# Re-ordering the first two rows of a three-stage macaron block: turned-tile copies as a step of their own, stores on ScalarE, three chunks kept on chip

## The chip, the core and the metric

The kernel runs on one core of a Trainium2 chip. The metric is device time in microseconds (us) of one execution, taken as the median of several runs. The engines have the profile's names: PE is TensorE, DVE is VectorE, ACT is ScalarE, POOL is GpSimd, SP is the sync engine, which in this kernel only issues transfers. Each engine works through its own queue in order.

## The reference

Eight rows (batch entries) of 512 tokens by 512 features go through feed-forward, attention, feed-forward, each with a layer norm before it and a residual around it. The change touches the first feed-forward. Cut to that:

```python
def ternary_quant(w, g=64):                      # per group of 64, in bf16
    scale = clip(mean(abs(w_g)), 1e-8)
    return clip(round(w_g / scale), -1, 1) * scale
def ffn(x, w_gate_up, w_proj):                   # hidden width 2048
    gate, up = split(x @ ternary_quant(w_gate_up).T, 2)
    h = silu(gate) * up
    h = h * rsqrt(mean(h * h) + eps)             # rms norm over the hidden width
    return h @ ternary_quant(w_proj).T
x = x + 0.5 * ffn(layernorm(x), w_gate_up, w_proj)
x = x + sliding_window_attention(layernorm(x))   # 32 heads, window 128
x = x + 0.5 * ffn(layernorm(x), w_gate_up, w_proj)
```

## The kernel before

Three stages follow one another: feed-forward "a", attention "b", feed-forward "c". Tiles with `_a` and `_c` in their names belong to the two feed-forwards. In a feed-forward the hidden width is cut into 16 chunks of 128 (`FC` = 16). For one row and chunk, `gate_or_up` (L283) makes gate and up with eight matmuls of 128x512 each (the normalised row is held as two terms, a rounded high one and the low rest). `silu` (L296) runs on ScalarE, `product` (L301) multiplies on VectorE into `h`. `high_term` (L306, ScalarE) and `low_term` (L311, VectorE) split `h` into `hs`, and `project` (L319) adds the chunk to the four output tiles with eight matmuls. The rms norm is a factor per token, so it is applied at the end, in `finish` (L335), from sums of the squares of `h`. All of the first stage's matmuls of the second and later rows find the quantised weights on chip.

The first two rows are different: `first_rows` (L362) quantises the weights while it computes rows 0 and 1. A class `Quantised` (L114) holds the steps for one weight tile. There are 16 gate/up tiles (`g[c]`, one a chunk) and 8 projection tiles (`pr[u]`, one for two chunks), each 128 partitions by 1024. The steps are `load` (DMA issued by SP), `magnitude` and `sign` (ScalarE), `scales` (VectorE, group means), `spread` (ScalarE, means copied to the groups' width, written to `step`), `first_half` and `second_half` (VectorE, five operations, giving `wt`), and `turned`: eight transposes on TensorE into a PSUM tile, its copy to the weight tile by ScalarE, and a store of that tile to DRAM for stage "c", issued by SP.

In `first_rows` the order on PE, DVE and ACT is the order of the program text (`manual_schedule`, L370); SP and POOL are ordered by the planner. The main loop (L422) runs over `c`. Pass `c` computes chunk `c` of row 0 and chunk `d = c - BEHIND` of row 1, with `BEHIND` = 5; it quantises tile `g[c + 1]` to its end and begins `g[c + 2]`, and works on one projection tile for each two passes. Row 0's sums of squares are made by four small matmuls a pass into the PSUM tile `ms_first` (L474). Row 0's projection runs `LAG` = 2 passes behind. Row 1's own layer norm is spread over the first passes (`norms[1]`: statistics, scaling, and the transposes with their copies). Row 1's `h` goes to DRAM (`h_kept`, L464), because the projection of row 1 can start only when row 0's outputs have left their four PSUM banks. After the loop a second loop (L494) reads those 16 chunks back, splits them and projects them, while row 2's layer norm is made beside it.

PSUM is full: four banks of outputs, two of gate and up, and two of a pool `ps_tr` for everything turned. `ms_first` holds one of these two for the whole of the loop. `work_tile` (L293) gives five 128x512 buffers for silu, `h`, squares and read-back chunks; `hs` has three.

The middle of pass `c` reads, in the order in which the engines get it:

```python
if not odd and 0 < u <= FC // 2:
    pr[u - 1].turned()
if d >= 0:
    up1 = gate_or_up(1, d, 1)
if c < FC:
    if c + 1 < FC:
        g[c + 1].turned()
    low_term(h0, hs[c])
    sq0 = work_tile("sq", 0, c)
    nc.scalar.activation(sq0, h0, AF.Square)
```

Of the kernel before, what the change touches and what calls it, by code (L numbers as in the profile page):

```python
# [24 lines left out]
def macaron_block(  # L25
# [88 lines left out]
    class Quantised:  # L114
# [59 lines left out]
        def turned(self):  # L174
            pt = self.ps_tr.tile(
                [P, len(self.blocks), P], BF16, tag="tr", name=f"ptq_{self.name}"
            )
            for n, (i, k) in enumerate(self.blocks):
                nc.tensor.transpose(pt[:, n, :], self.wt[:, i, k * P : (k + 1) * P], ident16)
            nc.scalar.copy(self.dst, pt)  # L180
            nc.sync.dma_start(self.kept, self.dst.bitcast(F32))

    def quantise_gate_up(stage, ps_tr, wgu, c):
        src = w_gate_up.rearrange("(i c p) d -> c p i d", i=2, p=P)[c]
# [62 lines left out]
    def ffn_stage(kind, source, target, first):  # L247
# [68 lines left out]
                ps_acc.tile([P, D], F32, tag="acc", name=f"o_{kind}{b}_{t}") for t in range(TB)  # L316
            ]

        def project(ops, e, hs):  # L319
            for t in range(TB):  # L320
                for part in range(2):
                    nc.tensor.matmul(  # L322
                        ops[t], hs[:, part, t * P : (t + 1) * P], wp[e // 2][:, e % 2, :],
                        start=(e == 0 and part == 0), stop=(e == FC - 1 and part == 1),
                    )

        def sums_of(b, sumsq):
# [4 lines left out]
                )  # L332
            return ms

        def finish(b, ops, ms):  # L335

            xt = xts[b]
            var = small.tile([P, TB], F32, tag="var", name=f"var_{kind}{b}")
            nc.vector.tensor_scalar(var, ms, 1.0 / FF, RMS_EPS, ALU.mult, ALU.add)
            rms = small.tile([P, TB], F32, tag="rstd", name=f"rms_{kind}{b}")  # L340
            inv_sqrt(rms, var)
            half = small.tile([P, TB], F32, tag="half", name=f"half_{kind}{b}")
            nc.vector.tensor_scalar(half, rms, 0.5, None, ALU.mult)
# [18 lines left out]
        def first_rows():  # L362


            BEHIND = TB + 1
            own = ExitStack()
            ms = ps_tr.tile([P, TB], F32, tag="tr", name="ms_first")
            stage = own.enter_context(tc.tile_pool(name="stage", bufs=1))
            engines = {
                mybir.EngineType.PE, mybir.EngineType.DVE, mybir.EngineType.Activation,  # L370
            }
            own.enter_context(tc.manual_schedule(engines=engines))
            g = [quantise_gate_up(stage, ps_tr, wgu, c) for c in range(FC)]
# [17 lines left out]
            def normed(b, t):  # L391

                if t < TB:
                    norms[b][1](t)
                if t >= 1:
                    norms[b][2](t - 1)

            row_loaded(0)
            waiting.pop(0).load()
            waiting.pop(0).load()  # L400
            row_loaded(1)
            for t in range(TB):
                norms[0][0](t)
            begun(g[0])
            g[0].scales()
            g[0].spread()
            for t in range(TB + 1):
                normed(0, t)
                if t == 1:
                    begun(g[1])  # L410
                if t == 2:
                    g[0].first_half()
            g[0].second_half()
            g[0].turned()
            g[1].scales()
            g[1].spread()
            begun(pr[0])

            ops = outputs(0)
            sumsq = work.tile([P, T], F32, tag="ss", name="ss_second", bufs=1)  # L420
            hs, square = {}, None
            for c in range(FC + BEHIND):  # L422
                u, odd, d = c // 2, c % 2 == 1, c - BEHIND
                if c < FC:
                    gate0 = gate_or_up(0, c, 0)
                    up0 = gate_or_up(0, c, 1)
                    if c + 2 < FC:
                        g[c + 2].magnitude()
                    sg0 = silu(0, c, gate0)
                    if c + 2 < FC:  # L430
                        signed(g[c + 2])
                    if c + 1 < FC:
                        g[c + 1].first_half()
                        g[c + 1].second_half()
                    h0 = product(0, c, up0, sg0)
                    hs[c] = high_term(0, c, h0)
                    if odd:
                        pr[u].first_half()
                    else:
                        pr[u].scales()  # L440
                if d >= 0:
                    gate1 = gate_or_up(1, d, 0)
                if not odd and 0 < u <= FC // 2:
                    pr[u - 1].turned()
                if d >= 0:
                    up1 = gate_or_up(1, d, 1)
                if c < FC:
                    if c + 1 < FC:
                        g[c + 1].turned()
                    low_term(h0, hs[c])  # L450
                    sq0 = work_tile("sq", 0, c)
                    nc.scalar.activation(sq0, h0, AF.Square)
                    if c + 2 < FC:
                        g[c + 2].scales()
                if d >= 0:
                    sg1 = silu(1, d, gate1)
                if c < FC:
                    if not odd:
                        pr[u].spread()
                    if c + 2 < FC:  # L460
                        g[c + 2].spread()
                if d >= 0:
                    h1 = product(1, d, up1, sg1)
                    nc.sync.dma_start(h_kept[d], h1)  # L464

                    square = sumsq if d == 0 else work_tile("sq", 1, d)
                    nc.scalar.activation(square, h1, AF.Square)
                if c < FC:
                    if odd:
                        pr[u].second_half()  # L470
                        if u + 1 < FC // 2:
                            begun(pr[u + 1])
                    for t in range(TB):
                        nc.tensor.matmul(  # L474
                            ms[:, t : t + 1], sq0[:, t * P : (t + 1) * P], ones,
                            start=(c == 0 and t == 0), stop=(c == FC - 1 and t == TB - 1),
                        )
# [10 lines left out]
                if d >= 1:  # L488
                    nc.vector.tensor_tensor(sumsq, sumsq, square, ALU.add)


            ops = outputs(1)
            kept, terms = {}, {}
            for e in range(-4, FC):  # L494
                if e + 4 < FC:
                    kept[e + 4] = work_tile("back", 1, e + 4)
                    nc.sync.dma_start(kept[e + 4], h_kept[e + 4])
                if 0 <= e + 2 < FC:
                    terms[e + 2] = high_term(1, e + 2, kept[e + 2])
                    low_term(kept.pop(e + 2), terms[e + 2])  # L500
                if e >= 0:
                    project(ops, e, terms.pop(e))
                if e == 1:
                    stored(0)
                    ms = sums_of(1, sumsq)
                spread_norm(2, e, 2)
            finish(1, ops, ms)
            own.close()

        def row(b):  # L510
# [3 lines left out]
            for c in range(FC + LAG):  # L514
# [20 lines left out]
            finish(b, ops, sums_of(b, sumsq))  # L535
            stored(b)

        if first:
# [340 lines left out]
```

## Time and profile before

| | us |
|---|---|
| median of 3 runs (2542.94 to 2548.51) | 2548.26 |
| the profiled execution | 2547.95 |
| its span, first to last instruction | 2546.1 |
| busy in the span: PE, DVE, ACT, POOL | 2440.0, 1324.2, 983.5, 909.2 |
| gate and up matmuls of stage "a" (2048) | 493.7 |
| projection matmuls of stage "a" (1024) | 269.4 |
| weight tile store, issue to landing, median | 2.6 |
| `h_kept` store and `back` load, issue to landing, median | 2.0, 3.4 |

A row of the profile names the engine, the source line, the operation and `out<-in`; "idle before" is the time in which that engine did nothing ahead of the row, followed by what ended it. Matmuls overlap, so busy time divided by count is the cost of one (493.7 / 2048 = 0.241 us), while the mean duration that the page lists is longer. The granted clock is the share of full speed that TensorE was given. DMA share is the mean busy share of the core's 16 DMA engines. `ptq` are turned weight tiles, `ptn` turned tiles of the layer norm, `wgu` and `wp` the weight tiles, `o` outputs.

### The profile page before, as it was taken

Reading aid. Unit: us, or ns where it says so; the run is one execution under the profiler, and the core shown is the slowest. Engines: PE = TensorE matmul, PEld = TensorE weight load, DVE = VectorE, ACT = ScalarE, POOL = GpSimd, SP = SyncE. Lnnn points to the kernel's source line nnn. Section 1 sums busy time; section 2 is a strip of 40 time slices with the busy share of each in tenths; the row PEclk is TensorE's granted clock in tenths of the full one; section 3 lists DMA queues with packets and bytes.
Section 4 is the critical chain, followed back from the end, with each engine's and each line's share of the span. In section 5 each row is a group of like instructions: output and inputs, shape, how many; then the busy total and the mean of one; then the engine's idle time right before and its main releaser. Section 6 shows DMA issues by size and latency. Waiting matters only on the chain.

```text
span 2546.1 us, 40511 instructions
## 1 busy us (share of the span) xinstructions
PE 2440.0 (96%) x16184; PEld 1788.0 (70%) x16184; DVE 1324.2 (52%) x3803; ACT 983.5 (39%) x1476; POOL 909.2 (36%) x778
## 2 busy tenths in 40 slices
PE   4889999999999999999999999998899999999998
PEld 3677788888888555555555555555688888888887
DVE  6665544434443466666666666665334444443442
ACT  5564322222222155555555555555222222222221
POOL 0000154444445233333333333333245445444444
PEclk9889999999999999999999999999899999999999
DMA  4332400000011100010110000022400000000000
GB/s 149 108 136 87 144 6 34 33 1 34 34 50 66 50 2 22 22 35 19 38 35 22 18 22 18 22 91 73 145 1 34 34 22 13 34 33 1 34 17 17
DMA packets 43564, 111.65 MB, mean 44 GB/s; under 512 B 3440, under 2 KB 7536, under 8 KB 40304
## 3 DMA queue, kind: packets, MB, share of 16 engines
q1 hardware_dynamic: 33392, 83.90, 9.2%
q10 hardware_dynamic: 9984, 25.17, 3.0%
q8 instruction: 127, 2.08, 0.4%
q14 instruction: 61, 0.50, 0.1%
HBM read 67.11 MB, written 41.94 MB: 43 GB/s over the span
## 4 chain that ended last, share of the span: by engine, by line
PE 92%; DVE 3%; ACT 2%; DMA 1%; issue 1%; POOL 0%; SPq 0%; POOLq 0%; DVEq 0%; ACTq 0%
PE gu_c L287 18%; PE gu_a L287 18%; PE o_a L322 10%; PE o_c L322 9%; PE sm L665 5%; PE sp L697 5%; PE wk L611 5%; PE av L733 4%; PE wq L611 4%; PE wo L611 4%; PE wv L611 4%; PE abT L751 1%; PE neg L683 1%; PE ptn_a L232 1%; PE ptn_b L232 1%
## 5 line engine op out<-in xcount | busy, mean ns | idle before, releaser
L287 PE MATMUL gu_a<-xs_a,wgu_a 128*128 128x512 f32 x2048 | 493.7, 395 | 1.8 <-ACT wgu_a L180 1.1
L287 PE MATMUL gu_c<-xs_c,wgu_c 128*128 128x512 f32 x2048 | 490.9, 393 | 0.7 <-ACT xs_c L235 0.7
L717 POOL TENSOR_SCALAR_AFFINE_SELECT pT<-pT 128x1024 f32<-128x1024 f32 x224 | 241.7, 1099 | 594.6 <-ACT pT L712 594.6
L287 PEld LDWEIGHTS gu_a<-xs_a,wgu_a 128*128 128x128 f32 x2048 | 387.7, 191 | 83.4 <-ACT wgu_a L180 1.4
L287 PEld LDWEIGHTS gu_c<-xs_c,wgu_c 128*128 128x128 f32 x2048 | 383.6, 189 | 79.8 <-ACT xs_c L235 0.9
L674 DVE CUSTOM_DVE_ANT_0 seen<-sm,window 128x256 f32<-128x256 f32 (+1 forms) x1024 | 331.6, 387 | 144.7 <-PE sm L665 143.1
L322 PE MATMUL o_a<-wp_a,hs_a 128*128 128x512 f32 x1024 | 269.4, 410 | 4.7 <-ACT hs_a L308 4.7
L322 PE MATMUL o_c<-wp_c,hs_c 128*128 128x512 f32 x1024 | 251.5, 389 | 0.0
L531 POOL TENSOR_TENSOR sq_c<-h_c 128x512 f32<-128x512 f32 x120 | 124.9, 1041 | 316.0 <-DVE h_c L303 302.5
L322 PEld LDWEIGHTS o_a<-wp_a,hs_a 128*128 128x128 f32 x1024 | 201.6, 199 | 47.9 <-ACT hs_a L308 5.2
L303 DVE TENSOR_TENSOR h_c<-gu_c,sg_c 128x512 f32<-128x512 f32 x128 | 88.2, 689 | 281.3 <-PE gu_c L287 280.1
L710 ACT ACTIVATE pT<-sp 128x512 f32<-128x512 f32 (+1 forms) x384 | 181.1, 547 | 129.5 <-PE sp L697 129.5
L303 DVE TENSOR_TENSOR h_a<-gu_a,sg_a 128x512 f32<-128x512 f32 x128 | 88.3, 690 | 262.6 <-PE gu_a L287 236.4
L712 ACT ACTIVATE pT<-pT 128x2048 f32<-128x2048 f32 (+1 forms) x128 | 217.3, 1698 | 7.9 <-DVE pT L706 3.9
L322 PEld LDWEIGHTS o_c<-wp_c,hs_c 128*128 128x128 f32 x1024 | 192.2, 188 | 39.9
L532 POOL TENSOR_TENSOR ss_c<-ss_c,sq_c 128x512 f32<-128x512 f32 x120 | 192.1, 1601 | 8.9
L298 ACT ACTIVATE sg_c<-gu_c 128x512 f32<-128x512 f32 x128 | 76.5, 598 | 264.8 <-PE gu_c L287 249.4
L308 ACT CAST hs_c<-h_c 128x512 fp32r<-128x512 f32 x128 | 79.5, 621 | 250.1 <-DVE h_c L303 250.1
L531 POOL TENSOR_TENSOR sq_a<-h_a 128x512 f32<-128x512 f32 x90 | 94.1, 1045 | 228.9 <-DVE h_a L303 219.9
L298 ACT ACTIVATE sg_a<-gu_a 128x512 f32<-128x512 f32 x128 | 76.4, 597 | 237.5 <-PE gu_a L287 228.7
L312 DVE TENSOR_TENSOR hs_c<-h_c,hs_c 128x512 fp32r<-128x512 f32 x128 | 124.0, 969 | 83.1 <-ACT hs_c L308 83.1
L308 ACT CAST hs_a<-h_a 128x512 fp32r<-128x512 f32 x112 | 69.5, 621 | 210.9 <-DVE h_a L303 210.9
(136 smaller groups left out, 3110.5 us busy)
## 6 DMA issues: line engine op xcount, KB each, us to landing
wf_gu<-w_gate_up_dram SPq DMA_DIRECT2D x16, 512.0 KB, 3.6
wgu_kept<-wgu_a SPq DMA_DIRECT2D x16, 512.0 KB, 2.6
rows_a<-x_a ACTq DMA_DIRECT2D x8, 1024.0 KB, 4.0
x_b<-rows_a SPq DMA_DIRECT2D x8, 1024.0 KB, 5.0
xr<-rows_a ACTq DMA_DIRECT2D x32, 256.0 KB, 3.1
rows_b<-xr SPq DMA_DIRECT2D x32, 256.0 KB, 2.4
x_c<-rows_b SPq DMA_DIRECT2D x8, 1024.0 KB, 4.8
wgu_c<-wgu_kept SPq DMA_DIRECT2D x16, 512.0 KB, 6.4
```

What stands on the lines that cost most here:

```text
L287: nc.tensor.matmul(ps, wgu[c][:, i * DC + k, :], xss[b][:, part, k, :], start=(k == 0 and part == 0), stop=(k == DC - 1 and part == 1),)
L298: nc.scalar.activation(sg, gate, AF.Silu)
L303: nc.vector.tensor_tensor(h, up, sg, ALU.mult)
L308: nc.scalar.copy(hs[:, 0, :], h)
L322: nc.tensor.matmul(ops[t], hs[:, part, t * P : (t + 1) * P], wp[e // 2][:, e % 2, :], start=(e == 0 and part == 0), stop=(e == FC - 1 and ...
L531: nc.gpsimd.tensor_tensor(sq, h, h, ALU.mult)
L532: nc.gpsimd.tensor_tensor(sumsq, sumsq, sq, ALU.add)
L611: nc.tensor.matmul(ps, lhs, rhs, start=(n == 0), stop=(n == len(pairs) - 1))
L674: nc.vector.tensor_tensor_reduce(out=seen[:, : n * P], in0=tiles[g][:, h, : n * P], in1=window[:, (2 - n) * P :], scale=-1.0, scalar=3.4e3 ...
L710: nc.scalar.activation(under, tiles[g][:, :, : n * P], AF.Relu, scale=-1.0)
L712: nc.scalar.activation(seen, seen, AF.Exp, scale=-1.0)
L717: nc.gpsimd.affine_select(out=half, in_=half, compare_op=ALU.is_ge, fill=0.0, base=0, pattern=[[0, 2 * NG], [sign, P]], channel_multiplier ...
```

## The change

`turned` keeps only the transposes. A new step `copied` does the copy, and the store is issued by ScalarE:

```diff
             for n, (i, k) in enumerate(self.blocks):
                 nc.tensor.transpose(pt[:, n, :], self.wt[:, i, k * P : (k + 1) * P], ident16)
-            nc.scalar.copy(self.dst, pt)
-            nc.sync.dma_start(self.kept, self.dst.bitcast(F32))
+            self.pt = pt
+
+        def copied(self):
+            nc.scalar.copy(self.dst, self.pt)
+            nc.scalar.dma_start(self.kept, self.dst.bitcast(F32))
```

The first weight tile is loaded ahead of x, its quantising comes ahead of the row's normalising, and `ms_first` is taken only after that:

```diff
-            BEHIND = TB + 1
+            BEHIND = TB + 2
-            ms = ps_tr.tile([P, TB], F32, tag="tr", name="ms_first")
...
+            waiting.pop(0).load()
             row_loaded(0)
             waiting.pop(0).load()
-            waiting.pop(0).load()
+            begun(g[0])
             row_loaded(1)
+            g[0].scales()
+            g[0].spread()
+            begun(g[1])
+            begun(pr[0])
             for t in range(TB):
                 norms[0][0](t)
-            begun(g[0])
-            g[0].scales()
-            g[0].spread()
-            for t in range(TB + 1):
-                normed(0, t)
-                if t == 1:
-                    begun(g[1])
-                if t == 2:
-                    g[0].first_half()
+            g[0].first_half()
             g[0].second_half()
             g[0].turned()
-            g[1].scales()
+            g[0].copied()
+            for t in range(TB + 1):
+                if t < TB:
+                    norms[0][1](t)
+                if t == TB:
+                    g[1].scales()
+                if t > 0:
+                    norms[0][2](t - 1)
             g[1].spread()
-            begun(pr[0])
+            ms = ps_tr.tile([P, TB], F32, tag="tr", name="ms_first")
```

In the main loop the square and the low term of row 0 move up, and the copies move down, behind the spreads (`KEPT` is 3). Row 1's transposes come one pass after their scaling. The running sum of row 1's squares (`squares_added`) is added in the pass after:

```diff
                     hs[c] = high_term(0, c, h0)
+                    sq0 = work_tile("sq", 0, c)
+                    nc.scalar.activation(sq0, h0, AF.Square)
                     if odd:
                         pr[u].first_half()
                     else:
                         pr[u].scales()
+                    low_term(h0, hs[c])
+                squares_added()
+                if 0 <= c - 2 < TB:
+                    norms[1][2](c - 2)
                 if d >= 0:
                     gate1 = gate_or_up(1, d, 0)
                 if not odd and 0 < u <= FC // 2:
                     pr[u - 1].turned()
                 if d >= 0:
                     up1 = gate_or_up(1, d, 1)
-                if c < FC:
-                    if c + 1 < FC:
-                        g[c + 1].turned()
-                    low_term(h0, hs[c])
-                    sq0 = work_tile("sq", 0, c)
-                    nc.scalar.activation(sq0, h0, AF.Square)
-                    if c + 2 < FC:
-                        g[c + 2].scales()
+                if c + 1 < FC:
+                    g[c + 1].turned()
                 if d >= 0:
                     sg1 = silu(1, d, gate1)
+                if not odd and 0 < u <= FC // 2:
+                    pr[u - 1].copied()
                 if c < FC:
                     if not odd:
                         pr[u].spread()
                     if c + 2 < FC:
+                        g[c + 2].scales()
                         g[c + 2].spread()
                 if d >= 0:
                     h1 = product(1, d, up1, sg1)
-                    nc.sync.dma_start(h_kept[d], h1)
+                if c + 1 < FC:
+                    g[c + 1].copied()
...
+                    if d >= FC - KEPT:
+                        terms[d] = high_term(1, d, h1)
+                        low_term(h1, terms[d])
+                    else:
+                        nc.scalar.dma_start(h_kept[d], h1)
...
-                if 1 <= c <= TB:
+                if 0 <= c - 1 < TB:
                     norms[1][1](c - 1)
-                    norms[1][2](c - 1)
...
                 if c == FC + LAG:
-                    finish(0, ops, ms)
+                    factor = rms(0, ms)
+                if c == FC + LAG + 1:
+                    finish(0, ops, factor)
```

`rms` is the first half of the old `finish`, the factor per token. After the loop row 1 is projected in another order: first the three chunks whose terms stayed on chip, then the 13 from DRAM, three loads ahead. The sums of row 1 and its factor come in steps 3 and 4 of that loop, where both stood before at step 1 and at the end:

```diff
-            for e in range(-4, FC):
-                if e + 4 < FC:
-                    kept[e + 4] = work_tile("back", 1, e + 4)
-                    nc.sync.dma_start(kept[e + 4], h_kept[e + 4])
...
+            order = [*range(FC - KEPT, FC), *range(FC - KEPT)]
+            for n in range(KEPT):
+                kept[n] = work_tile("back", 1, n)
+                nc.sync.dma_start(kept[n], h_kept[n])
+            for n, e in enumerate(order):
+                if n >= 1 and n + 2 < FC:
+                    ahead = order[n + 2]
+                    terms[ahead] = high_term(1, ahead, kept[ahead])
+                    low_term(kept.pop(ahead), terms[ahead])
...
+                project(ops, e, terms.pop(e), order[0], order[-1])
```

`project` takes the first and last chunk of that order, for the start and stop of the accumulation.

More of the change, by code (lines that the diff above doesn't have):

```diff
@@ L317, in outputs, with project @@
             ]
-        def project(ops, e, hs):
+        def project(ops, e, hs, begin=0, end=FC - 1):
             for t in range(TB):
@@ L323, in project @@
                         ops[t], hs[:, part, t * P : (t + 1) * P], wp[e // 2][:, e % 2, :],
-                        start=(e == 0 and part == 0), stop=(e == FC - 1 and part == 1),
+                        start=(e == begin and part == 0), stop=(e == end and part == 1),
                     )
@@ L333, in sums_of, with rms, finish @@
             return ms
-        def finish(b, ops, ms):
-            xt = xts[b]
+        def rms(b, ms):
             var = small.tile([P, TB], F32, tag="var", name=f"var_{kind}{b}")
             nc.vector.tensor_scalar(var, ms, 1.0 / FF, RMS_EPS, ALU.mult, ALU.add)
-            rms = small.tile([P, TB], F32, tag="rstd", name=f"rms_{kind}{b}")
-            inv_sqrt(rms, var)
+            factor = small.tile([P, TB], F32, tag="rstd", name=f"rms_{kind}{b}")
+            inv_sqrt(factor, var)
+            return factor
+        def finish(b, ops, factor):
+            xt = xts[b]
             half = small.tile([P, TB], F32, tag="half", name=f"half_{kind}{b}")
-            nc.vector.tensor_scalar(half, rms, 0.5, None, ALU.mult)
+            nc.vector.tensor_scalar(half, factor, 0.5, None, ALU.mult)
             for t in range(TB):
@@ L389, in signed, with squares_added @@
                     waiting.pop(0).load()
[L391 to L396, printed above, removed]
+            waiting.pop(0).load()
             row_loaded(0)
             waiting.pop(0).load()
-            waiting.pop(0).load()
+            begun(g[0])
             row_loaded(1)
+            g[0].scales()
+            g[0].spread()
+            begun(g[1])
+            begun(pr[0])
             for t in range(TB):
                 norms[0][0](t)
-            begun(g[0])
-            g[0].scales()
-            g[0].spread()
-            for t in range(TB + 1):
-                normed(0, t)
-                if t == 1:
-                    begun(g[1])
-                if t == 2:
-                    g[0].first_half()
+            g[0].first_half()
             g[0].second_half()
             g[0].turned()
-            g[1].scales()
+            g[0].copied()
[6 more added lines that the diff above has]
+                    norms[0][2](t - 1)
             g[1].spread()
-            begun(pr[0])
+            ms = ps_tr.tile([P, TB], F32, tag="tr", name="ms_first")
             ops = outputs(0)
             sumsq = work.tile([P, T], F32, tag="ss", name="ss_second", bufs=1)
-            hs, square = {}, None
+            hs, kept, terms, squares = {}, {}, {}, []
+            def squares_added():
+                if squares:
+                    nc.vector.tensor_tensor(sumsq, sumsq, squares.pop(), ALU.add)
+            KEPT = 3
             for c in range(FC + BEHIND):
@@ L463, in first_rows @@
                     h1 = product(1, d, up1, sg1)
-                    nc.sync.dma_start(h_kept[d], h1)
-                    square = sumsq if d == 0 else work_tile("sq", 1, d)
-                    nc.scalar.activation(square, h1, AF.Square)
+                if c + 1 < FC:
+                    g[c + 1].copied()
+                if d >= 0:
+                    if d == 0:
+                        nc.scalar.activation(sumsq, h1, AF.Square)
+                    else:
+                        squares.append(work_tile("sq", 1, d))
+                        nc.scalar.activation(squares[0], h1, AF.Square)
+                    if d >= FC - KEPT:
+                        terms[d] = high_term(1, d, h1)
+                        low_term(h1, terms[d])
+                    else:
+                        nc.scalar.dma_start(h_kept[d], h1)
                 if c < FC:
@@ L486, in first_rows @@
                 if c == FC + LAG:
-                    finish(0, ops, ms)
-                if d >= 1:
-                    nc.vector.tensor_tensor(sumsq, sumsq, square, ALU.add)
+                    factor = rms(0, ms)
+                if c == FC + LAG + 1:
+                    finish(0, ops, factor)
+            squares_added()
             ops = outputs(1)
-            kept, terms = {}, {}
-            for e in range(-4, FC):
-                if e + 4 < FC:
-                    kept[e + 4] = work_tile("back", 1, e + 4)
-                    nc.sync.dma_start(kept[e + 4], h_kept[e + 4])
[L498 to L503, printed above, removed]
+            order = [*range(FC - KEPT, FC), *range(FC - KEPT)]
[7 more added lines that the diff above has]
+                    low_term(kept.pop(ahead), terms[ahead])
+                    if ahead + KEPT < FC - KEPT:
+                        kept[ahead + KEPT] = work_tile("back", 1, ahead + KEPT)
+                        nc.sync.dma_start(kept[ahead + KEPT], h_kept[ahead + KEPT])
+                project(ops, e, terms.pop(e), order[0], order[-1])
+                if n == 1:
                     stored(0)
+                if n == 3:
                     ms = sums_of(1, sumsq)
-                spread_norm(2, e, 2)
-            finish(1, ops, ms)
+                if n == 4:
+                    factor = rms(1, ms)
+                spread_norm(2, n, 2)
+            finish(1, ops, factor)
             own.close()
@@ L534, in row @@
                     project(ops, c - LAG, hs.pop(c - LAG))
-            finish(b, ops, sums_of(b, sumsq))
+            finish(b, ops, rms(b, sums_of(b, sumsq)))
             stored(b)
```

## The prediction

> **What bounds the kernel now.** I read the page's rows by slice first: TensorE is at 9 tenths in nearly all of the 40 slices, and the weak ones are at the start. So I cut the span where the first two rows end: the matmuls of row 2 begin at 306.77 us on the chain of waits. A table by stretch (columns: length, busy of TensorE, weight load, VectorE, ScalarE, GpSimd with instruction counts, granted clock, DMA share, GB/s):
>
> ```profile
> 25.80:109.40 83.60, 60.35 (x273) 49.20 (x274) 58.92 (x98) 50.58 (x63) 2.89 (x4) 0.80 0.32 117
> 109.40:244.60 135.20, 120.52 (x594) 97.32 (x593) 86.59 (x134) 76.22 (x101) 0.00 (x0) 0.91 0.32 117
> 244.60:306.80 62.20, 56.73 (x258) 45.88 (x257) 29.04 (x52) 19.04 (x31) 2.88 (x3) 0.97 0.40 131
> ...
> 306.80:2546.00 2239.20, 2197.20 (x15040) 1591.82 (x15039) 1135.20 (x3486) 827.87 (x1270) 900.70 (x762) 0.99 0.10 33
> ```
>
> After 306.8 TensorE is busy 98% at a clock of 0.99, and the change touches none of it: I carry those 2239 us over. Everything is decided before. There TensorE idles 83.60 - 60.35 = 23.3, 135.20 - 120.52 = 14.7 and 62.20 - 56.73 = 5.5 us, and part of its busy time runs at a low clock.
>
> The timeline of one loop pass (start, length, what; in brackets the idle time before it and what ended it):
>
> ```profile
> 129.58 0.62 PE L179 MATMUL ptq_gu<-ident,q_wt_gu 128*128 128x128 bf16 x8
> ...
> 130.24 1.01 ACT L180 CAST wgu_a<-ptq_gu 128x1024 fp32r<-128x1024 bf16 x1 [2.56 <-PE ptq_gu L179]
> ...
> 131.15 0.63 ACT L452 ACTIVATE sq_a<-h_a 128x512 f32<-128x512 f32 x1
> ...
> 131.83 1.05 PE L474 MATMUL ms_first<-ones,sq_a 128*128 128x1 f32 x8 [1.63 <-ACT sq_a L452]
> ...
> 132.75 3.59 PE L322 MATMUL o_a<-wp_a,hs_a 128*128 128x512 f32 x8
> ```
>
> The turned weight tile is copied, only then is row 0's product squared, and TensorE stands 1.63 us because its next instruction sums those squares. ScalarE had idled 2.56 us before the copy: the square waited for its place in the queue, not for data. Then eight projection matmuls take 3.59 us, against 1.96 in undisturbed passes. The clock says why (busy of TensorE, clock):
>
> ```profile
> 130.00:132.00 2.00, 0.37 (x6) 1.00 0.00 0
> 132.00:134.00 2.00, 2.00 (x11) 0.74 0.72 291
> 134.00:136.00 2.00, 2.00 (x6) 0.50 0.27 102
> ```
>
> In the passes ahead of row 1 (c = 0 to 4) the gaps are larger:
>
> ```profile
> 56.12 0.61 PE L179 MATMUL ptq_gu<-ident,q_wt_gu 128*128 128x128 bf16 x8 [1.95 <-ACT wp_a L180]
> ...
> 71.31 1.71 PE L474 MATMUL ms_first<-ones,sq_a 128*128 128x1 f32 x8 [2.48 <-ACT sq_a L452]
> ...
> 75.95 1.09 PE L232 MATMUL ptn_a<-ident,xn_a 128*128 128x128 f32 x4 [2.94 <-DVE xn_a L224]
> ...
> 272.85 5.68 PE L322 MATMUL o_a<-wp_a,hs_a 128*128 128x512 f32 x16 [4.75 <-ACT hs_a L308]
> ```
>
> The third is row 1's transpose, queued on TensorE in the pass in which VectorE only just makes its input. The fourth is the end of the loop: row 1's first chunk is fetched from DRAM behind the last store.
>
> **The passes c = 6 to 15, both rows running.** At full clock a pass costs what the chain shows for one without a gap: 32 gate and up matmuls 7.26, sums 0.79, projection 1.97 = 10.02; plus 0.48 where a gate/up tile is turned (not in c = 15), plus 0.46 for a projection tile in even passes. Ten passes: 100.2 + 9 x 0.48 + 5 x 0.46 = 106.8 us. They took 135.2: 14.7 idle and about 13.7 of low clock and handing over.
>
> The square now follows the high term directly, ahead of the sums by row 1's up matmuls (1.9 us): this gap goes. What is late next is the tile copy, now behind the spreads and followed by the next pass's gate matmuls. Even pass, 0 = gate start, with the spacing of back-to-back rows: up ends at 3.65; VectorE's product, behind 3.4 us of quantising, ends at 4.6; high term 5.2, square 5.7, row 1's silu 6.2, projection copy 7.2, its store's issue 7.6, two spreads 9.6 (the second needs VectorE's scales, about 8.6), copy 10.6. TensorE gets there at 10.96: 0.3 us of cover. Turning both weight tiles shares one free buffer, since the sums hold the other; the projection copy ends at 7.2, and the second turn is due at 7.7. Loads of two passes: TensorE 21.5; VectorE (2 x 3.4 quantising, 2 x 1.4 scales, 8 x 0.65 for products, low terms and sums, 4.7 for the projection tile) 19.5; ScalarE 16.4 plus issues. TensorE stays the bound; I allow 0.4 us a pass for handing over: 111 us, **24 less**.
>
> Here a rule speaks against. The Trainium skill, "TensorE: Matmul & The Clock Gate", section "Why this matters for your kernels", wants no TensorE gap above about 3 us; by it a gap of 1.63 costs no clock, and the passes would fall only by their 14.7 us idle, to 120.5. The row shows the clock at 0.50 right after 1.63 us of idle and 1.05 us of matmuls one column wide. I take the row.
>
> **Stores on ScalarE.** 24 weight stores and 13 of row 1 leave SP's queue; 3 stores and 3 loads vanish. The issue is 0.32 to 0.34 us on SP and 0.33 for ScalarE's own row store. 37 x 0.33 = 12 us go to an engine 56% busy in the loop. Behind a store on ScalarE stand the spread or the next magnitude; the spread's readers are next pass's quantising and, after it, the copy. A weight store also waits for its own copy; I charge about 0.5 us each, inside the sum above. Whether a store also waits for an older transfer no ScalarE row here shows: from nothing to a full landing of 2.6 us (the weight store's median). I take nothing, since the built order asks only for transfers some passes old. SP gains: loads no longer stand behind a store waiting for ScalarE, but outside the start no magnitude waited for its weights, so 0. The skill ("DMA: Bandwidth & Descriptors", "Issuing engines are not separate DMA queues") would charge only issue time on whichever sequencer; the sum would then be 0 with ScalarE under its limit.
>
> **The start.** The first weights landed at 8.9, behind x; loaded first, with the 3.6 us of such a load, at about 4.5. Then VectorE is the line: scales to 6.9, statistics and the constants to 11.2, quantising 14.6, then four normalise, copy and low-term steps in turn with TensorE and ScalarE, and the second tile's scales (1.4) ahead of the last low term: 23.7 against 25.77, **2 less**. If ScalarE, which now takes the third tile's magnitude and sign before the first copy, must wait for that load (it cannot land much before 10.8), this gain halves.
>
> **The passes c = 0 to 5.** Row 1 starts a pass later, so six passes instead of five run without it, with nothing to cover the new order. c = 0: up ends 6.15 after the gate start (cold clock, as now); product 0.7; projection scales 1.35; low term 0.65; scales 1.35; spread 1.0; copy 1.0: the next gate starts 12.3 after, where it took 10.0. **That pass loses 2.3.** The later ones gain, because the transpose's input is a pass old. c = 3: 12.0 for up end + product 0.7, first half 1.35, two low terms 1.3, turn 0.6, what is left of the scales beside it 0.8, spread and copy 2.0 = 6.8, plus some 5 us for gate and up partly at half clock; it took 15.9. In even passes transposed tile, projection tile and gate/up tile go through the one buffer in turn, about 14. Gate starts:
>
> | pass | 0 | 1 | 2 | 3 | 4 | 5 | 6 |
> |---|---|---|---|---|---|---|---|
> | now | 25.8 | 35.8 | 48.8 | 64.4 | 80.3 | 95.4 | 109.4 |
> | estimate | 23.7 | 36.0 | 47.5 | 62.5 | 74.5 | 88.5 | 100.5 |
>
> Gaps of 3 us remain here, so I leave the clock at half for part of each. Bounds on this stretch: no gain at all (9 worse), or warm clock (5 better).
>
> **The end.** c = 16 to 21: six passes of row 1 at 3.63, two projections 1.97 each, one turn 0.46: 26.2. Row 0's finish (half and four VectorE steps, 2.9) now also has a low term before it, and the next product waits: 1.5 on TensorE, where 0.72 shows now. Then 16 projections at 1.84, sums 0.8 and four transposes at 0.44: 32.0. Sum 59.7 against 62.2 now. The 4.75 us go (three chunks are on chip, 3 x 1.84 = 5.5 us cover the 2.8 us fetch), but one more pass stands there. **2.5 less.**
>
> **Sum.** 100.5 + 111 + 59.7 = 271.2 against 306.8: 35.6 less. The profiled execution took 2547.95 (span 2546.1); the median of the runs is 2548.26, the same for this purpose. 2548 - 36 = **2512**; its own range 2502 to 2526.
>
> **Rivals.**
> - *Late copies* (18%): the 0.3 us cover is too thin, each pass stands some 1.6 us for its weight tile. Ten times 1.6 is 16: 2528. For it: the copy is last in a ScalarE chain of eight steps; against: ScalarE has 5 us in two passes free.
> - *All gaps go* (13%): the early passes also stay warm and the handing over costs nothing: 5 + 4 + 1.5 less, some 2501. Against: VectorE's chain is unavoidable in c = 0 to 5.
> - *Stores hold ScalarE* (5%), the slower side. If each issue blocks ScalarE until the older transfer lands (2.6 us, five in two passes), two passes cost ScalarE 16.4 + 5 x 3.0 = 31.4 where they last 27.0 now: ten passes 157, and the early gain of 9 goes: 2548 + 22 - 4 = 2566. It decides from (27.0 - 16.4)/5 = 2.1 us per store upward.
> - *The order is not what the text says* (2%): were the copy still ahead of the square, nothing moves: 2545. Against: the instruction order of the built kernel has square, spreads, copy.
>
> The likeliest holds 62%. Range for 8 in 10: 2498 to 2531. Within 0.3% (7.6 us, about what a measurement can tell) is same: faster 0.93, same 0.03, slower 0.04.
>
> **What would show it.** In the new profile: no gap before the sums in c above 5, projection groups near 2.0 us, clock near 1.0 in the middle stretch; the second gate start near 36, no earlier than now; no fetch wait after the loop. A wait of gate matmuls for the tile copy, or ScalarE idle at a store, would prove me wrong.

## The result, and the profile after

| | before | after |
|---|---|---|
| median of the runs, us | 2548.39 (2542.94 to 2549.95) | 2513.73 (2510.46 to 2518.49) |
| the profiled execution, us | 2547.95 | 2518.49 |
| its span, us | 2546.1 | 2516.5 |
| matmuls of row 2 begin at, us | 306.77 | 275.50 |

The ratio is 0.9869, with a 95% interval of 0.9848 to 0.9891: 28 to 39 us less. 2512 had been forecast. The profile of after is that of the slowest of its four runs.

The table by stretch of the new kernel has the columns of the prediction's table and is cut at the same passes (first gate matmuls, pass 6, pass 16, row 2). Pass 16 computes row 1's chunk 10 here, where it computed chunk 11 before, because row 1 starts a pass later:

```profile
22.00:106.40 84.40, 60.77 (x257) 49.49 (x257) 60.41 (x102) 48.14 (x59) 2.89 (x4) 0.76 0.27 100
106.40:216.05 109.65, 108.74 (x593) 88.33 (x592) 84.53 (x130) 76.88 (x101) 0.00 (x0) 1.00 0.39 144
216.05:275.50 59.45, 58.11 (x273) 47.78 (x272) 30.14 (x56) 19.89 (x33) 3.41 (x3) 1.00 0.33 115
...
275.50:2516.50 2241.00, 2197.91 (x15041) 1592.60 (x15039) 1134.20 (x3485) 828.06 (x1270) 900.39 (x761) 0.99 0.10 33
```

The middle stretch fell from 135.20 to 109.65 us: idle time from 14.7 to 0.9, the clock from 0.91 to 1.00. The first stretch takes 84.40 where it took 83.60, though it holds 16 matmuls fewer (row 1's first chunk has left pass 5), and its clock fell from 0.80 to 0.76. The rest of the kernel took 2241.0 against 2239.3. Over the profiles of this study the same rest took between 2233.5 and 2241.0, so a difference of a few us is better read from the time at which row 2 begins than from the medians. That time has a spread too: run 9 below has the program of the changed kernel up to pass 16 and begins that pass at 217.95 instead of 216.05, so some 2 us in a single profile say little.

From the timeline, the projection of pass 7, the pass shown of before, and then pass 8, an even one like that of the prediction's sum:

```profile
126.19 2.10 PE L325 MATMUL o_a<-wp_a,hs_a 128*128 128x512 f32 x8
...
136.19 0.62 PE L179 MATMUL ptq_gu<-ident,q_wt_gu 128*128 128x128 bf16 x8
...
136.65 1.00 PE L496 MATMUL ms_first<-ones,sq_a 128*128 128x1 f32 x8
...
137.52 2.10 PE L325 MATMUL o_a<-wp_a,hs_a 128*128 128x512 f32 x8
137.88 1.01 ACT L183 CAST wgu_a<-ptq_gu 128x1024 fp32r<-128x1024 bf16 x1
...
138.92 0.33 ACTq L184 DMA_DIRECT2D wgu_kept<-wgu_a  x1
```

The sums follow the transposes with no idle time. In pass 7 the projection takes 2.10 instead of 3.59 us. (In before, six of the nine passes with a gap had such a slow projection; pass 8 was one of the other three.) The copy runs beside the projection. It ends at 138.89, and the next gate matmuls start at 139.45: half a microsecond of cover.

What waits in the passes without row 1, and at the end of the loop:

```profile
35.19 5.43 PE L290 MATMUL gu_a<-xs_a,wgu_a 128*128 128x512 f32 x16 [2.69 <-ACT wgu_a L183]
...
56.50 0.61 PE L179 MATMUL ptq_p<-ident,q_wt_p 128*128 128x128 bf16 x8 [2.94 <-DVE xs_a L239]
...
60.11 3.76 PE L325 MATMUL o_a<-wp_a,hs_a 128*128 128x512 f32 x8
...
241.70 2.11 PE L290 MATMUL gu_a<-xs_a,wgu_a 128*128 128x512 f32 x8 [1.34 <-DVE h_a L306]
```

The second gate start stands 2.69 us for the late copy, and the third, at 46.72, stands 3.01. In passes 2 to 5 the weight tile's transposes stand 2.94 us for the low term of row 1's transposed tile, which holds the one free bank; the projection behind them runs at half clock. The fetch wait of 4.75 us is gone. Row 0's finish holds row 1's product for 1.34 us, where it held it for 0.72 before.

### The profile page after: what moved, and what is told of

It reads as the page before. It is cut to its first block, busy times and chain, and to the rows that moved or that the text cites. A ratio compares the mean times of both kernels' runs of the same rounds, so it can differ in the third digit from the quotient of the medians.

```text
span 2516.5 us, 40486 instructions
## 1 busy us (share of the span) xinstructions
PE 2431.4 (97%) x16184; PEld 1782.1 (71%) x16184; DVE 1322.7 (53%) x3803; ACT 984.8 (39%) x1476; POOL 909.8 (36%) x778
## 3 DMA queue, kind: packets, MB, share of 16 engines
q8 instruction: 127, 2.08, 0.3%
## 4 chain that ended last, share of the span: by engine, by line
PE 93%; DVE 3%; ACT 2%; issue 1%; DMA 1%; POOL 0%; ACTq 0%; POOLq 0%; DVEq 0%; SPq 0%
PE gu_c L290 19%; PE gu_a L290 18%; PE o_a L325 9%; PE o_c L325 9%; PE sm L692 5%; PE sp L724 5%; PE av L760 5%; PE wk L638 5%; PE wq L638 4%; PE wo L638 4%; PE wv L638 4%; PE abT L778 1%; PE neg L710 1%; PE ptn_b L235 1%; PE oTp L800 1%
## 5 line engine op out<-in xcount | busy, mean ns | idle before, releaser
L325 PE MATMUL o_a<-wp_a,hs_a 128*128 128x512 f32 x1024 | 259.0, 399 | 0.0
L325 PEld LDWEIGHTS o_a<-wp_a,hs_a 128*128 128x128 f32 x1024 | 195.2, 192 | 40.3
```

Of the source, the lines that this page charges most:

```text
L325: nc.tensor.matmul(ops[t], hs[:, part, t * P : (t + 1) * P], wp[e // 2][:, e % 2, :], start=(e == begin and part == 0), stop=(e == end and ...
```

## The experiments

Each run has the runs of the kernel before beside it on the same chip; the ratio to them is given with its 95% interval. L numbers in rows are those of the kernel that ran.

**1. Only the square moved.** The kernel before, with row 0's square put directly behind the high term and nothing else changed:

```diff
                     hs[c] = high_term(0, c, h0)
+                    sq0 = work_tile("sq", 0, c)
+                    nc.scalar.activation(sq0, h0, AF.Square)
...
                     low_term(h0, hs[c])
-                    sq0 = work_tile("sq", 0, c)
-                    nc.scalar.activation(sq0, h0, AF.Square)
```

> The kernel before with one edit: row 0's square directly behind the high term, the tile copy left where it was. Mine (the square's place is what made the sums wait): the 1.63 us gap and the half clock behind it go in the passes with both rows, the stretch from pass 6 to row 1's pass 11 falls from 135 to about 111 us, the kernel to 2522 to 2528. Rival (the copy as a late step of its own and the stores on ScalarE carry the gain): little moves, 2540 or above.

Measured: 2517.34 us, 0.9873 (0.9854 to 0.9891), below the 2522 to 2528 that I had expected. The runs cannot tell it from the whole change. By stretch, from pass 6 and from pass 16 (row 1's chunk 11):

```profile
104.10:217.00 112.90, 110.76 (x593) 88.51 (x592) 88.71 (x138) 77.72 (x104) 0.00 (x0) 1.00 0.40 144
217.00:280.06 63.06, 57.69 (x257) 46.56 (x256) 28.96 (x52) 19.04 (x31) 2.58 (x3) 0.95 0.39 130
```

The middle fell to 112.90 at full clock, with the copy still early and the stores on SP. Passes 0 to 5 fell too, from 83.6 to 78.5 us (25.59 to 104.10), which my range had left out. Row 2 starts at 280.06, 4.6 us behind the whole change. So what the rest of the change adds is small and of both signs: passes 6 to 15 take 3.3 us less than here and the end 3.6 less, but pass 6 starts 2.3 us later. In odd passes here a product comes late and the up matmuls of row 1 stand 0.5 us for it.

**2. The square put back behind the copy,** copy and stores left late:

```diff
                     hs[c] = high_term(0, c, h0)
-                    sq0 = work_tile("sq", 0, c)
-                    nc.scalar.activation(sq0, h0, AF.Square)
...
                 if c + 1 < FC:
                     g[c + 1].copied()
+                if c < FC:
+                    sq0 = work_tile("sq", 0, c)
+                    nc.scalar.activation(sq0, h0, AF.Square)
```

> The changed kernel with the square put back behind the gate/up tile's copy, copy and stores left late as they are. Mine: the gap ahead of the sums returns, and larger, since the copy is now later than before (about 2 us more): passes 6 to 15 take 130 us or more, the kernel 2535 to 2555. Rival (the late copies carry the gain): at most 5 us above the changed kernel, 2519.

Measured: 2590.44 us, 1.0168 (1.0149 to 1.0187). The direction was as expected, the size was not. Passes 0 to 5, which I had not counted, take 103.7 us instead of 84.4, with gaps ahead of the sums of up to 6.75. Passes 6 to 15 take 164.0 us, and every pass but the last shows this in its timeline (the table's row for these passes stands first):

```profile
126.50:290.50 164.00, 135.22 (x593) 109.89 (x592) 83.81 (x129) 77.33 (x100) 0.00 (x0) 0.81 0.26 93
...
138.62 1.86 PE L497 MATMUL ms_first<-ones,sq_a 128*128 128x1 f32 x8 [3.10 <-ACT sq_a L478]
140.35 3.76 PE L325 MATMUL o_a<-wp_a,hs_a 128*128 128x512 f32 x8
```

The gap is 2.2 to 3.7 us, and now sums and projection run at half speed in all nine of these passes, while behind a gap of 1.63 the projection had been slow in six of nine. So the late copy by itself is no gain; it is harmful unless the square leaves its shadow.

**3. Stores issued by SP again:** in `copied` and for `h_kept`, `nc.scalar.dma_start` became `nc.sync.dma_start`.

> The changed kernel with the 37 stores issued by SP again. Mine (TensorE is the bound and each store costs ScalarE some 0.4 us under that limit): the same, 2511 to 2517. Rival A (stores on SP hold up weight loads behind them): slower by 5 or more. Rival B (stores hold ScalarE on the path of the late copies): faster by 5 or more.

Measured: 2511.06 us, 0.9861 (0.9842 to 0.9879), and row 2 starts at 275.57 against 275.50: the same. What the issue costs ScalarE can be read from the waits of the changed kernel, ScalarE's behind a copy (total, times, longest):

```profile
ACT sq_a L484 <- ACT wgu_a L183: 3.2, 8, 0.4
...
ACT q_step_p_p L155 <- ACT wp_a L183: 2.0, 5, 0.4
```

A store costs 0.4 us of ScalarE between two instructions: waiting for its own copy and the issue. In this run, with the stores on SP, these waits of ScalarE behind a copy are gone, and the time is the same: the cost is real, and hidden. No store held ScalarE for the landing of an older one.

**4. Useless matmuls in the gap.** The kernel before, with the sums' tile made a full bank wide; the results of the added matmuls go to columns that nothing reads:

```diff
+                    if 0 < c < FC - 1:
+                        for n in range(7):
+                            nc.tensor.matmul(
+                                ms[:, 32:512], wgu[c][:, n, :], xss[0][:, 0, 0, 32:512],
+                                start=False, stop=False,
+                            )
                     for t in range(TB):
                         nc.tensor.matmul(
                             ms[:, t : t + 1], sq0[:, t * P : (t + 1) * P], ones,
```

> The kernel before with seven useless 128x480 matmuls (1.5 us) ahead of the sums in passes 1 to 14, in the gap where TensorE waits for the square; their results go to unused columns of the sums' bank. No useful work is added or taken away. If the clock falls because of that gap: the projection groups behind it take 2.0 instead of 3.5 us, the stretch from pass 6 falls by about 10 us of its 135, the kernel to 2533 to 2540. If a gap below 3 us costs no clock: no gain, 2548 to 2552.

Measured: 2526.40 us, 0.9918 (0.9900 to 0.9935). Ninety-eight matmuls that compute nothing made the kernel some 21 us faster, more than I expected. By the profiles 16.5 us of this arise ahead of row 2, which starts at 290.28; the rest lies in the untouched part and its spread. Passes 6 to 15 took 124.2 us at a clock of 1.00 (135.20 at 0.91), passes 0 to 5 78.7 (83.6). The stretch, and a pass in the timeline:

```profile
104.07:228.23 124.16, 123.73 (x657) 99.78 (x656) 87.52 (x136) 77.85 (x103) 0.00 (x0) 1.00 0.35 128
...
124.70 1.77 PE L475 MATMUL ms_first<-xs_a,wgu_a 128*128 128x480 f32 x7
126.53 1.05 PE L480 MATMUL ms_first<-ones,sq_a 128*128 128x1 f32 x8
127.44 2.09 PE L322 MATMUL o_a<-wp_a,hs_a 128*128 128x512 f32 x8
```

The sums start as late as they did, but the projection behind them takes 2.09. That is the clock alone: about 11 of the 25.6 us that the change gained in these passes.

**5. Row 1's transposed tiles at the end of the pass.**

```diff
-                if 0 <= c - 2 < TB:
-                    norms[1][2](c - 2)
...
                 if 0 <= c - LAG < FC:
                     project(ops, c - LAG, hs.pop(c - LAG))
+                if 0 <= c - 2 < TB:
+                    norms[1][2](c - 2)
```

> The changed kernel with row 1's transposed layer-norm tiles (passes 2 to 5) moved from ahead of the weight tiles' transposes to the end of the pass, behind the projection. Mine (they hold the one free bank of turned tiles until VectorE's low term, and the weight tile's transposes stand 2.9 us for it): the four waits of 2.9 us go, passes 2 to 5 take 8 to 12 us less than 59.6, the kernel 2502 to 2507. Rival (VectorE's own work sets these passes): less than 3 us, 2511 to 2515.

Measured: 2508.60 us, 0.9852 (0.9836 to 0.9869). Row 2 starts at 271.33, 4.2 us earlier. Passes 2 to 5 take 54.0 us instead of 59.6. The waits of 2.94 went, but others took their place:

```profile
56.17 0.61 PE L179 MATMUL ptq_gu<-ident,q_wt_gu 128*128 128x128 bf16 x8 [2.47 <-ACT wp_a L183]
...
66.39 0.62 PE L179 MATMUL ptq_gu<-ident,q_wt_gu 128*128 128x128 bf16 x8 [1.10 <-DVE q_wt_gu L172]
```

In even passes the second tile still stands for the first one's copy; in odd passes VectorE's quantising is now late. The gain in these passes, 5.6 us, is about half of what I had expected, and the median missed the range that I had given: VectorE's own work, the rival, had a part too.

**6. As 5, and the copy ahead of the spreads while row 1 is not running.**

```diff
+                if d < 0:
+                    g[c + 1].copied()
                 if c < FC:
                     if not odd:
                         pr[u].spread()
...
-                if c + 1 < FC:
+                if d >= 0 and c + 1 < FC:
                     g[c + 1].copied()
```

> As the run before, and in the passes without row 1 (0 to 5) the gate/up tile's copy ahead of the two spreads. Mine (the copy waits for VectorE's scales through the spreads, with no matmul of row 1 to cover it): the second gate start falls from 35.2 to about 32, passes 0 to 5 take another 4 to 8 us less, the kernel 2496 to 2503, faster than both. Rival (the spread on time matters more, since VectorE's next quantising waits for it): no gain over the run before.

Measured: 2505.20 us, 0.9842 (0.9828 to 0.9857). Row 2 starts at 264.89, 10.6 us ahead of the change; the median falls less and misses the 2496 to 2503 that I had expected. From run 5 the medians hardly separate it, the profile does (6.4 us at row 2). The second gate start is at 31.55 instead of 35.19:

```profile
31.55 3.94 PE L290 MATMUL gu_a<-xs_a,wgu_a 128*128 128x512 f32 x16
37.44 1.04 PE L179 MATMUL ptq_gu<-ident,q_wt_gu 128*128 128x128 bf16 x8 [1.95 <-DVE q_wt_gu L172]
...
50.82 0.78 PE L179 MATMUL ptq_gu<-ident,q_wt_gu 128*128 128x128 bf16 x8 [3.92 <-ACT wp_a L183]
```

Gate matmuls no longer wait for the copy of their tile. The next in line are VectorE's quantising and, in passes 2 and 4, the copy of the projection tile, for which the second tile's transposes stand 3.92 and 2.58 us.

**7. Row 1 a pass earlier** (`BEHIND = TB + 1`).

> The changed kernel with row 1 starting in pass 5 again, as in the kernel before. Mine: one pass without row 1 (13.2 us) and one of row 1 alone (3.6) become one with both (10.7 plus 3 us of waiting for the last transposed tile): about 3 us less, 2508 to 2513. Rival (the extra pass of distance is needed): 2516 or more.

Measured: 2517.53 us, 0.9889 (0.9875 to 0.9904); row 2 starts at 276.26. No gain, as the rival said. Pass 5, now with both rows, takes 16.5 us, because row 1's first gate matmuls stand for the tile turned in the same pass; that is 3.3 more than without row 1. The end is only 2.9 us shorter (56.6 against 59.45):

```profile
100.08 0.50 PE L290 MATMUL gu_a<-xs_a,wgu_a 128*128 128x512 f32 x1 [2.07 <-ACT xs_a L238]
100.95 5.30 PE L290 MATMUL gu_a<-xs_a,wgu_a 128*128 128x512 f32 x15 [0.37 <-DVE xs_a L239]
```

**8. x loaded ahead of the first weight tile again.**

```diff
-            waiting.pop(0).load()
             row_loaded(0)
             waiting.pop(0).load()
+            waiting.pop(0).load()
             begun(g[0])
```

> The changed kernel with x loaded ahead of the first weight tile again. Mine: ScalarE gets the tile at 8.9 instead of 4.2, VectorE does statistics meanwhile only if they do not stand behind the scales, which they do: first and second gate start both some 4 us later, the kernel 2516 to 2519. Rival (the start is hidden by what follows): second gate start unchanged at 35.2, 2512 to 2515.

Measured: 2519.25 us, 0.9897 (0.9882 to 0.9912). ScalarE gets the tile at 8.58 instead of 4.18; the second gate start moves from 35.19 to 39.18 and row 2's from 275.50 to 281.85. In the changed order the load is on the path: it is worth about 4 us there, and the new order of the start would have been a loss without it.

**9. No chunk kept on chip.** All 16 go to DRAM and are read back in the order and with the lead of the kernel before:

```diff
-                    if d >= FC - KEPT:
-                        terms[d] = high_term(1, d, h1)
-                        low_term(h1, terms[d])
-                    else:
-                        nc.scalar.dma_start(h_kept[d], h1)
+                    nc.scalar.dma_start(h_kept[d], h1)
...
```

> The changed kernel with no chunk of row 1 kept on chip: all 16 go to DRAM (stores on ScalarE) and are read back in order 0 to 15, as in the kernel before. Mine (the fetch wait comes from reading back at all): about 4.7 us of TensorE waiting return at the start of the second loop, row 2 starts near 279, the kernel 2516 to 2519. Rival (the wait came from SP's queue, where the first load stood behind the last store; with stores on ScalarE it is gone anyway): row 2 starts within 1.5 us of 275.5, the kernel 2511 to 2515.

Measured: 2519.92 us, 0.9890 (0.9876 to 0.9904), an interval that overlaps that of the change. Row 2 starts at 279.90, but 1.9 us of the 4.4 arose before the end. The end itself takes 61.95 against 59.45. Its first load, and the first projection of row 1:

```profile
243.10 7.15 SPq L513 DMA_DIRECT2D back_a<-h_kept  x7
244.17 0.69 DVE L306 TENSOR_TENSOR h_a<-gu_a,sg_a 128x512 f32<-128x512 f32 x1 [1.15 <-PE gu_a L290]
...
246.35 0.49 PE L325 MATMUL o_a<-wp_a,hs_a 128*128 128x512 f32 x1 [2.28 <-ACT hs_a L311]
```

The load is issued before the last product. In the kernel before it came 1.2 us after the last product's start (269.36 against 268.21), behind the last store in SP's queue. So about half of the wait of 4.75 us was probably SP's order, which falls with the move of the stores alone. (Runs 1 and 4, with the stores on SP, still have 4.65; but run 9 differs from them in more than the stores.) The kept chunks save 2.3 us of waiting and three small stops of 0.2 to 0.3. On the other side, their own low term delays row 0's finish: the 1.34 is gone in this run. Net the end is 2.5 us longer without them, less than the 4.7 that I had expected and more than the rival's 1.5. This rests on one profile of each kernel; their medians do not separate them.

**10. Useless matmuls in 6,** where TensorE waits for a weight tile in passes 1 to 5 (the sums' tile is a bank wide again, as in 4):

```diff
+                if d < 0 and c > 0:
+                    for n in range(4 if odd else 10):
+                        nc.tensor.matmul(
+                            ms[:, 32:512], wgu[c][:, n % 8, :], xss[0][:, 0, 0, 32:512],
+                            start=False, stop=False,
+                        )
                 if c + 1 < FC:
                     g[c + 1].turned()
```

> The fastest order so far (transposed tiles last, copy first) with useless 128x480 matmuls, 10 in even and 4 in odd passes from 1 to 5, where TensorE waits ahead of the gate/up tile's transposes. If low clock still costs there: projection groups of passes 2 to 5 take about 2.0 instead of 3.76 us, row 2 starts 4 to 8 us before 264.9, the kernel 2497 to 2502. If VectorE sets these passes, the clock gain is waited away: within 2 us of 2505.

Measured: 2499.63 us, 0.9813 (0.9800 to 0.9827), the fastest kernel of the study. Row 2 starts at 262.64, only 2.3 us earlier than in 6 and short of the 4 to 8 expected. By stretch, passes 0 to 5 and 6 to 15:

```profile
22.90:91.60 68.70, 57.01 (x287) 45.91 (x288) 55.31 (x93) 44.08 (x56) 2.89 (x4) 0.90 0.35 123
91.60:203.20 111.60, 109.56 (x596) 88.30 (x595) 88.31 (x137) 79.44 (x104) 0.00 (x0) 1.00 0.39 142
```

The clock rose from 0.79 to 0.90 in the early passes; only the projections of passes 3 and 5 ran at full speed (2.08 and 2.10), those of 2 and 4 still took 3.76 and 3.67. Passes 0 to 5 take 3.6 us less than in 6 (68.7 against 72.3), and 1.4 us of this are lost again in passes 6 to 15: part of the gain is waited away, as the second expectation said. The rest of the difference in the median lies in the untouched part (2233.5 us in this profile), which I do not explain.

## Why the prediction was right, and where it was not

The time was 2513.7 where 2512 had been said, and the likeliest case was the one that came. That the two lie so close is in part luck. In the profiles row 2 begins 31.3 us earlier, not 35.6; the medians differ by 34.7, and the few us between are spread from run to run. By its steps, in the profiled execution:

| step | predicted | measured |
|---|---|---|
| first gate start | 23.7 | 21.26, then 22.86 for the other 15 matmuls |
| second gate start | 36.0 | 35.19 |
| third gate start (pass 2) | 47.5 | 46.72 |
| pass 6 starts | 100.5 | 106.36 |
| passes 6 to 15 | 111 | 109.7 |
| the end | 59.7 | 59.45 |
| row 2 starts | 271.2 | 275.50 |

**The square and the clock: right, and shown.** Run 1 has the gain with the square alone, run 2 loses it and more with the square alone put back, and run 4 separates the clock from the gap. The Trainium skill's rule of a 3 us gap ("TensorE: Matmul & The Clock Gate", "Why this matters for your kernels"), as the prediction read it and weighed it against the row, fell: 1.63 us of idle with eight one-column matmuls behind it cost 11 us in ten passes. Had I gone by it, I would have been about 11 us too high there (120.5 against 109.7).

**The stores: right.** Nothing by run 3. The mechanism of the slower rival, a store holding ScalarE until an older one lands, does not occur: ScalarE stood 0.4 us per weight store, and the sum had 0.5.

**The late copies: cover of 0.3 us predicted, 0.5 measured** in the pass shown; from pass 6 on TensorE never waits for a copy. The rival of late copies falls. A wait of gate matmuls for the tile copy, which I had named as a sign of being wrong, does stand at the second and third gate starts (2.69 and 3.01 us), where the sum of pass 0 had the copy last as well; from pass 6 on there is none.

**The start and pass 0: right in sign and size.** The start came 3 us earlier and pass 0 took it back. Run 8 shows the load to be worth 4 us in this order, and run 6 that the lost time lay in the copy behind the spreads. Two slips do not matter here: the terms given for pass 0 add up to 12.2, not 12.3, and pass 2 stands at 15.0 in the table of gate starts, where the text says about 14.

**Passes 2 to 5: the term that was mis-sized.** I had put 53 us from the third gate start to pass 6 (47.5 to 100.5); they took 59.6 (46.7 to 106.4), each of the four passes 1.2 to 2.0 us longer than estimated. The queue for the one free bank was in the sum. Its price was not: TensorE stands 2.94 us in each of the four passes, and what I had charged as "some 5 us for gate and up partly at half clock" leaves out that the sums and the projection behind such a wait are slow as well, 1.6 to 1.8 instead of 0.8 and 3.6 to 3.8 instead of 2.0. Run 5 shows the queue by taking it away: 5.6 us less in these passes, 4.2 at the start of row 2. What the low clock costs there is not measured apart in the changed kernel; in the order of run 6, filling the gaps gave 3.6 us in passes 0 to 5.

**The end: the sum was right, its reason half right.** The finish's stall was put at 1.5 and is 1.34. The fetch wait I gave wholly to the chunks kept on chip; run 9 suggests that about half of it went with the stores' leaving SP's queue.

## What to carry to other kernels

When TensorE waits on a small reduction, look first at the place of its input's producer in that engine's queue: one instruction moved up, past a tile copy or two, brought nearly all that the whole re-ordering did. Price a TensorE gap by the granted clock behind it, not by its length; useless wide matmuls in an unavoidable gap can pay. An order that costs nothing where other matmuls cover it (copy last) costs time in the first passes, where nothing does.

## What the runs showed of the hardware that I had not expected

Work for nothing can save time: 98 matmuls of 128x480 in gaps of 1.6 to 2.5 us took the kernel from 2547.5 to 2526.4 us, as the clock of ten passes rose from 0.91 to 1.00.

A gap's length alone does not give its price. With 1.63 us ahead of the sums, six of nine projection groups ran slow (3.2 to 3.8 us); with 2.2 to 3.7 us in run 2 all nine did, and the sums too (1.86 instead of 1.05). The shortest of run 2's gaps, 2.21 us, has transposes ahead of it and the one-column sums behind it. Run 9 has a gap of about the same length, 2.28 us, between full-width matmuls. The tables by stretch behind the two, run 2 first, show the clock (third number from the end):

```profile
276.00:278.00 2.00, 2.00 (x6) 1.71 (x7) 0.00 (x0) 0.00 (x0) 0.00 (x0) 0.50 0.16 60
...
246.00:248.00 2.00, 1.42 (x5) 0.97 (x6) 0.94 (x2) 0.29 (x1) 0.00 (x0) 1.00 0.84 293
```

This suggests that the narrow work around a gap counts nearly as idle time for the clock. It is one pair of gaps, and no run varied the width of the sums, so it is not shown.
